# Layer 0 of a graph network: chunks turned so that one scan goes over five or ten features, and ScalarE turns the sums back

## The chip, the cores and the metric

The kernel runs on one core of a Trainium2 chip. The metric is the device time of one execution in microseconds (us); less is better. The core has five engines that run side by side, each with its own queue of instructions in a fixed order: TensorE (PE), VectorE (DVE), ScalarE (ACT), GpSimd (POOL) and SyncE (SP). Transfers between the device memory (DRAM) and the on-chip memory (SBUF) are issued from the queues of SP, ACT and POOL. PSUM is the small memory that PE writes and that DVE and ACT can also read and write.

## The reference

Four graph layers follow each other on 12500 nodes with 64 features and 200000 edges, sorted by destination. Layer 0, the one that is changed, computes per edge a message and per node a mean:

```python
h = jnp.maximum(_layernorm(x), 0.0)
msg = node_feats[src] + edge_feats                      # node_feats = h, edge_feats [200000, 64]
agg_sum = jax.ops.segment_sum(msg, dst, num_segments=N)
agg_mean = agg_sum / jnp.maximum(deg, 1.0)[:, None]
h = (1.0 + eps[0]) * node_feats + agg_mean
h = jax.nn.relu(_batchnorm(h @ W1 + b1, gamma1, beta1))
h = jax.nn.relu(_batchnorm(h @ W2 + b2, gamma2, beta2))
```

The other layers also gather rows by `src` and sum them by `dst`; they are not changed.

## The kernel before

**Sums by scan.** The edges are sorted by destination, so all edges of a node form a run. A range of edges is laid out as 128 partitions with TS slots each. For one feature, a scan along the slots of a partition adds up a run: `state = on * state + m`, where `on` (`goes_on`) is 1 where the edge has the same destination as the one before it, else 0. The last slot of a run then holds the node's sum. The scanned values go to a table `run_sums_0` in DRAM, and later the row of each node's last edge is gathered from it. `carry_on` adds what goes over from one partition to the next, by a scatter on POOL (L307).

**Two passes in layer 0.** `Runs` objects hold the slots. `cold` has 1001 slots per partition in 21 chunks of 48: POOL gathers the `h` row of each edge's source (L299, one indirect transfer per slot, 128 rows of 64 values, tile `m_src`, `rows_ahead = 3` buffers), SP loads the edge features (`m_edge`, pieces of 16 slots), ACT copies eight slots of them to PSUM (`ps_e`, L1519, one buffer), DVE adds them (L1520), and scans the chunk (L792). `hot` has the first 578 slots per partition in 19 chunks of 32: SP loads only edge features (`m_hot`), and DVE scans them; what the source rows contribute there is computed with matrix products of 0/1 blocks (below). A chunk lies in SBUF as slots by features, so the 48 (or 32) values of one feature are 64 values apart, and there are 64 scans per chunk, one per feature:

```python
for d in range(D):
    nc.vector.tensor_tensor_scan(m[:, :nt, d], on, m[:, :nt, d],
        0.0 if before is None else before[:, d : d + 1], op0=ALU.mult, op1=ALU.add)
```

`before` (L834 for cold, L1585 for hot) is the chunk's last slot, which the next chunk starts from. The mask `on` is copied to PSUM by ACT (`ps_masks`, L785), 240 or 256 slots at a time. Then ACT's queue issues the chunk's store to `run_sums_0` (L837, L1586).

**Beside the cold chunks.** `edge_pass` loops over the cold chunks, and after each it lets four other works go on as far as they are due: the hot chunks (`hot_features`, due evenly over the first six cold chunks), `counts.work` (100 counts for degrees and run ends: ACT L930 and L946, DVE L931, PE L938), the zeroing of a table (`by_edge<-zeros`, 195 transfers on ACT's queue), and `build` of 13 blocks. `build` unpacks edges (L1212 to L1244, all between cold chunks 4 and 6), and then makes one-hot tiles on DVE (`part_is`, `place_is`, L1324 and L1332), multiplies them on PE (`ps_a`, L1368), and casts them on ACT into a block (L1382). `sums_of_block` then loads the split source rows in tiles of 14 (`split_rows`, L1302, `JA = 14`, seven per block, two buffers), multiplies them by the block on PE (`ps_h`, L1304), and DVE adds up three parts (`hot_rows`, L1313). Each unit of the next block takes along one tile of these sums.

**Order.** Within an engine the order of instructions is fixed when the kernel is built, and works are interleaved there: an instruction that waits holds all behind it on its engine. Tiles with one buffer (`bufs=1`) are written again only when all readers of their last contents are done.

**End of the stage.** After cold chunk 20, `carry_on` runs, POOL scatters its rows, and then gathers `sum` rows, with which the first matrix products of layer 0 begin.

Of the kernel before, what the change touches and what calls it, by code (L numbers as in the profile page):

```python
# [18 lines left out]
P = 128  # L19
D = 64  # L20
# [5 lines left out]
J = 98  # L26
# [28 lines left out]
JA = 14  # L55
# [105 lines left out]
def kernel(  # L161
# [30 lines left out]
    nc = tc.nc  # L192
# [527 lines left out]
    class Runs:  # L720
# [1 line left out]

        def __init__(self, keep, scratch, psum, edges, name, size, row0=0):
# [7 lines left out]
            self.src_i = edges.sources(keep, name)  # L733
            self.dst_i, dst_f, before_f = edges.destinations(scratch, name)
            self.dst_f = dst_f

            self.goes_on = keep.tile([P, self.TS], F32, name=f"{name}_goes_on")
# [10 lines left out]
        def first_runs(self, keep, pool, psum):  # L748
# [25 lines left out]
            nc.vector.memset(self.carry[:, 1, :1], 0.0)  # L774
            nc.vector.tensor_mul(self.carry[:, 1, 1:], one[:, : P - 1], self.carry[:, 0, 1:])

        def mask(self, psum, t0, nt):


            at = t0 % self.mask_width  # L780
            if at == 0:
                n = min(self.mask_width, self.TS - t0)
                if psum is not None:
                    self.on = psum.tile([P, 512], F32, name="ps_on")
                nc.scalar.copy(self.on[:, :n], self.goes_on[:, t0 : t0 + n])  # L785
            return self.on[:, at : at + nt]

        def scan(self, m, on, before, nt):


            for d in range(D):
                nc.vector.tensor_tensor_scan(  # L792
                    m[:, :nt, d],
                    on,
                    m[:, :nt, d],
                    0.0 if before is None else before[:, d : d + 1],
                    op0=ALU.mult,
                    op1=ALU.add,
                )

        def edge_pass(self, table, load, message, beside=(), masks=1, ends=1, late=False):
# [3 lines left out]
            with ExitStack() as stack:  # L805
                pool = stack.enter_context(tc.tile_pool(name="edges", bufs=2))
                psum = stack.enter_context(tc.tile_pool(name="ps_edge", bufs=1, space=PSUM))
                self.psum = psum
# [16 lines left out]
                for c, (t0, nt) in enumerate(self.chunks):  # L825
                    on, loaded = ahead
                    if c + 1 < len(self.chunks):
                        ahead = load_chunk(*self.chunks[c + 1])
                    m = message(pool, psum, loaded, on, t0, nt)
                    if not masks:  # L830
                        on = self.mask(None, t0, nt)
                    self.scan(m, on, before, nt)
# [154 lines left out]
    class Ordered(Edges):  # L987
# [56 lines left out]
        def prepare(self, keep, edge_keep):  # L1044

            pool = self.scratch_pool
            with self.scratch, tc.tile_pool(name="ps_prepare", bufs=1, space=PSUM) as psum:
                self.cold = Runs(edge_keep, pool, psum, cold_edges, "cold", self.SIZE_0, self.COLD)
                self.hot = Runs(edge_keep, pool, psum, hot_edges, "hot", self.HOT_SIZE_0)
# [247 lines left out]
        def sums_of_block(self, pool, psum, block, b):  # L1297

            p = psum.tile([P, 3, D], F32, name="ps_h")
            for j0 in range(0, J, JA):  # L1300
                a = pool.tile([P, JA, 3, D], BF16, name="split_rows")
                nc.sync.dma_start(a, self.split[:, j0 : j0 + JA])  # L1302
                for j in range(j0, j0 + JA):
                    nc.tensor.matmul(  # L1304
                        p.rearrange("p k d -> p (k d)"),
                        block[:, j, :],
                        a[:, j - j0].rearrange("p k d -> p (k d)"),
                        start=j == 0,
                        stop=j == J - 1,
                    )  # L1310
                yield
            r = pool.tile([P, D], F32, name="hot_rows")
            nc.vector.tensor_reduce(r, p.rearrange("p k d -> p d k"), AX.X, ALU.add)  # L1313
            nc.sync.dma_start(self.hot_sums_0[b * CB : (b + 1) * CB], r)
# [168 lines left out]


        SIZE_0 = 48
        HOT_SIZE_0 = 32

        def layer0(self, h0):
            PIECE = 16
# [22 lines left out]

            def message(pool, psum, s, on, t0, nt):
                e = cold.pop(t0)
                for b in range(0, nt, TE):
                    nb = min(TE, nt - b)
                    p = psum.tile([P, TE * D], F32, name="ps_e").rearrange("p (t d) -> p t d", d=D)
                    at = b % PIECE
                    self.copied = nc.scalar.copy(p[:, :nb, :], e[b // PIECE][:, at : at + nb, :])  # L1519
                    nc.vector.tensor_add(s[:, b : b + nb, :], s[:, b : b + nb, :], p[:, :nb, :])  # L1520
                t1 = t0 + nt
                if t1 < self.cold.TS:
                    cold[t1] = pieces(pool, t1, min(self.SIZE_0, self.cold.TS - t1))
                return s

            def built(c):

# [5 lines left out]
            with self.first_stack:  # L1533
                self.prepare(self.count_keep, self.edge_keep)
                with tc.tile_pool(name="ps_masks", bufs=1, space=PSUM) as psum:
                    on = psum.tile([P, 2, 256], F32, name="ps_masks")
                    for k, runs in enumerate((self.hot, self.cold)):
                        runs.on = on[:, k, :]
                        runs.mask_width = 256 // runs.size * runs.size
# [28 lines left out]
        def hot_features(self):  # L1568

            runs = self.hot  # L1570
            with tc.tile_pool(name="hot_features", bufs=2) as pool:
# [31 lines left out]
        def layer1(self, a_table, b_table):  # L1603
# [5 lines left out]
            def load(pool, on, t0, nt):  # L1609
# [16 lines left out]
                self.all.scan(d, on, prior[0], nt)  # L1626
# [353 lines left out]
```

## Time and profile before

| | us |
|---|---|
| median of 3 runs (6052.3 to 6059.85) | 6053.1 |
| the profiled execution | 6051.88 |
| its span, first to last instruction | 6050.0 |
| first gather of layer 0 starts | 74.2 |
| last gather of layer 0 starts | 1392.2 |
| scatter that ends the layer's edge pass starts | 1459.5 |

In the stretch from 60 to 1480 us the scans of cold chunks take 283 us of DVE (1216 of 128x48 at 291 ns, 64 at 231, 64 of 128x41 at 277), counted one by one, and the scans of hot chunks 211 us.

How to read the views: a group is a line of the kernel with an engine and an operation; after the count come its busy time in us, the mean ns of one, and the idle time of the engine just before it with what ended that idle time. The waits list who waited for whom, in us, times, and the longest. In the timeline each piece has its start and duration in us; the part in brackets is the idle time before it. In the slices, each digit is the busy share in tenths in one of 40 equal parts of the span (151 us each). `PEld` is PE's weight load. Instructions on DVE overlap by some tens of ns, so that scans in a row take less than the sum of their durations.

### The profile page before, as it was taken

What the parts mean: (1) busy time and instruction counts of PE and PEld (TensorE: products, weight loads), DVE (VectorE), ACT (ScalarE), POOL (GpSimd) and SP (SyncE); (2) the same over time, 40 slices, a digit from 0 to 9 for tenths busy, and PEclk for the clock granted to TensorE, in tenths of its full rate; (3) what the DMA queues carried; (4) which work ended last, traced back from release to release, by engine and by line L of the source; (5) the groups of instructions that cost most, each with busy time, mean ns of one, the idle gap of its engine ahead of it and who ended that gap; (6) DMA issues with size and microseconds to landing.
All of it is one profiled execution on the core that took longest, in us unless ns stands there. A gap on an engine that the chain in (4) does not pass through costs nothing. (4 is left out here: it accounts for less than half of the span.)

```text
span 6050.0 us, 59020 instructions
## 1 busy us (share of the span) xinstructions
PE 3615.4 (60%) x16229; PEld 1736.4 (29%) x16229; DVE 3500.5 (58%) x12505; ACT 1680.2 (28%) x3570; POOL 4155.7 (69%) x4378
## 2 busy tenths in 40 slices
PE   3412665664646145455555556559995899659995
PEld 2101443442232011111111111134444444344444
DVE  6799988775525278677877777642333223352333
ACT  2421465554327032233444434320001000020001
POOL 5777677774436767777777777567776677647775
PEclk9999887776655577666666666559996899769995
DMA  6573477785113244344444444439995899659993
GB/s 207 203 268 99 158 262 257 256 282 174 38 65 105 77 153 141 119 140 159 147 147 149 164 145 137 146 97 385 386 386 184 328 385 386 245 192 386 386 381 125
DMA packets 452864, 1277.60 MB, mean 211 GB/s; under 512 B 136677, under 2 KB 146855, under 8 KB 427434
## 3 DMA queue, kind: packets, MB, share of 16 engines
q1 hardware_dynamic: 247274, 925.85, 41.6%
q0 software_dynamic: 139872, 143.10, 9.8%
q10 hardware_dynamic: 65376, 204.79, 8.8%
q8 instruction: 130, 2.13, 0.1%
q14 instruction: 212, 1.74, 0.1%
HBM read 859.98 MB, written 418.12 MB: 211 GB/s over the span
## 5 line engine op out<-in xcount | busy, mean ns | idle before, releaser
L299 POOL DMA_INDIRECT m_src<-ordered_a_table,all_src_i x1563 | 1475.6, 944 | 502.3 <-issue 458.9
L792 DVE TENSOR_TENSOR_SCAN m_src<-ps_on,before,m_src 128x32 f32<-128x32 f32 (+3 forms) x4032 | 805.2, 281 | 1041.5 <-DMA m_src<-ordered_h,later_src_i 346.1
L299 POOL DMA_INDIRECT m_src<-ordered_h,cold_src_i x1001 | 963.8, 963 | 318.8 <-issue 297.1
L1382 ACT CAST block<-ps_a 128x294 bf16<-128x294 f32 (+3 forms) x1801 | 859.7, 535 | 773.3 <-PE ps_a L1368 707.3
L1368 PE MATMUL ps_a<-place_is,part_is 128*128 128x98 bf16 (+4 forms) x2671 | 736.5, 375 | 472.1 <-DVE place_is L1332 204.1
L1703 PE MATMUL ps_upper<-blocks,upper 128*128 128x512 bf16 x3822 | 873.5, 380 | 154.5 <-DMA blocks<-blocks 133.2
L703 PE MATMUL ps_e<-w1e,et 64*128 64x512 f32 x392 | 284.3, 813 | 513.0 <-DVE m_src L714 512.9
L1703 PEld LDWEIGHTS <-upper 128*128 128x128 bf16 x3822 | 377.1, 99 | 619.2 <-issue 231.9
L1324 DVE TENSOR_TENSOR part_is<-ps_iota,part 128x512 bf16<-128x512 f16 (+2 forms) x665 | 424.4, 638 | 212.7 <-PE ps_a L1368 192.3
L1368 PEld LDWEIGHTS <-part_is 128*128 128x128 bf16 x2671 | 286.4, 121 | 902.6 <-issue 334.0
L299 POOL DMA_INDIRECT m_src<-ordered_scaled,later_src_i x430 | 405.7, 944 | 187.0 <-issue 129.5
L299 POOL DMA_INDIRECT m_src<-ordered_h,later_src_i x430 | 405.8, 944 | 158.7 <-issue 129.8
L938 PE MATMUL ps_row<-digits,on 128*128 128x391 bf16 x1016 | 299.8, 434 | 352.2 <-DVE on L931 135.8
L299 POOL DMA_INDIRECT m_src<-ordered_v,later_src_i x430 | 405.8, 944 | 146.1 <-issue 129.5
L1712 PE MATMUL ps_lower<-blocks,lower 128*64 128x512 bf16 x3822 | 464.5, 382 | 0.0
L1332 DVE TENSOR_SCALAR place_is<-ps_iota,place 128x294 bf16<-128x294 f16 (+3 forms) x1199 | 446.7, 428 | 0.0
L792 DVE TENSOR_TENSOR_SCAN m_dst<-ps_on,last_dst,m_dst 128x64 f32<-128x64 f32 (+1 forms) x1536 | 372.5, 323 | 0.0
L714 DVE TENSOR_TENSOR m_src<-m_src,ps_e 128x512 f32<-128x512 f32 x196 | 133.7, 682 | 390.1 <-DMA m_src<-ordered_a_table,all_src_i 207.1
L711 PE MATMUL ps_e<-m_dst,ident 128*128 128x512 f32 x392 | 281.2, 807 | 122.0 <-DVE m_dst L792 122.0
L1726 ACT COPY sum<-ps_upper 128x512 f32<-128x512 f32 x39 | 22.8, 585 | 1009.9 <-PE ps_upper L1703 878.3
L792 DVE TENSOR_TENSOR_SCAN m_src<-ps_masks,before,m_src 128x48 f32<-128x48 f32 (+1 forms) x1280 | 273.0, 290 | 0.2
L1712 PEld LDWEIGHTS <-lower 128*64 128x64 bf16 x3822 | 193.2, 109 | 255.6 <-issue 115.7
(364 smaller groups left out, 4413.2 us busy)
## 6 DMA issues: line engine op xcount, KB each, us to landing
blocks<-blocks SPq DMA_DIRECT2D x273, 1792.0 KB
blocks<-block SPq DMA_DIRECT2D x52, 3136.0 KB
split_rows<-split SPq DMA_DIRECT2D x91, 672.0 KB
by_edge<-zeros ACTq DMA_DIRECT2D x195, 256.0 KB
m_dst<-by_edge SPq DMA_DIRECT2D x24, 2048.0 KB
run_sums<-m_src ACTq DMA_DIRECT2D x24, 2048.0 KB
run_sums<-m_src ACTq DMA_DIRECT2D x39, 1024.0 KB
run_sums<-m_src ACTq DMA_DIRECT2D x20, 1536.0 KB
```

What stands on the lines that cost most here:

```text
L299: nc.gpsimd.indirect_dma_start(out=t, out_offset=None, in_=table, in_offset=bass.IndirectOffsetOnAxis(ap=idx, axis=0),)
L703: nc.tensor.matmul(p[:, :nb, :], et[: nb * EF], w1e[: nb * EF, : nb * D], start=True, stop=more is None,)
L711: nc.tensor.matmul(p[:, :nb, :], ident, more[:, b : b + nb, :], start=False, stop=True)
L714: nc.vector.tensor_add(m[:, b : b + nb, :], m[:, b : b + nb, :], p[:, :nb, :])
L792: nc.vector.tensor_tensor_scan(m[:, :nt, d], on, m[:, :nt, d], 0.0 if before is None else before[:, d : d + 1], op0=ALU.mult, op1=ALU.add,)
L938: nc.tensor.matmul(p[:, b, :W], on[:, 0, :], self.digits[:, i, v : v + W], start=i == 0, stop=i == 1,)
L1324: nc.vector.tensor_tensor(to[:, :n, :], iota[:, None, :m].to_broadcast([P, n, m]), of[:, t : t + n][:, :, None].to_broadcast([P, n, m]), o ...
L1332: nc.vector.tensor_scalar(place[:, k, :], iota[:, : J * w], self.place[:, t + k : t + k + 1], None, op0=ALU.is_equal,)
L1368: nc.tensor.matmul(out[:, :, (k - first) * w : (k - first + 1) * w], part[:, k, :], place[:, k, a * w : z * w], start=begin, stop=left == 0,)
L1382: nc.scalar.copy(block[:, a:z, c : c + wide], out)
L1703: nc.tensor.matmul(upper, self.upper[:, j].rearrange("p a d -> p (a d)"), a[:, :, j - j0, :], start=j == 0, stop=j == J - 1,)
L1712: nc.tensor.matmul(lower[k * D : (k + 1) * D], self.lower[:, j, :], a[:, :, j - j0, :], start=j < 2, stop=j >= J - 2,)
```

## The change

- `cold` and `hot` of layer 0 call `several_features`. Their chunks are scanned in a tile `turned` (64 x 48 values, one buffer, shared by hot and cold), in which a feature's slots lie side by side.
- Cold: DVE's adds write into `turned` in place of `m_src`, with slots 4 bytes and features 192 bytes apart. Hot: ACT copies the loaded chunk into `turned` first.
- One scan then goes over 5 features of 48 slots (cold, 13 scans per chunk, twelve of 240 values and one of 192) or 10 features of 24 slots (hot, 7 scans). The mask holds the chunk's `goes_on` once per feature, with 0 at each first slot; what the chunk before carries over is added into the first slot by one DVE operation (`before` times `goes_in`).
- ACT writes this mask for every chunk, and copies the scanned `turned` back into the chunk's own tile, from which it is stored.
- Hot chunks have 24 slots in place of 32: 25 chunks in place of 19.
- `split_rows` tiles have 7 rows in place of 14, so there are 14 transfers per block in place of 7, and each unit takes half as many products along.
- The sources of the hot edges, which nothing reads, are not loaded.

```diff
+        def several_features(self, keep, on):
+            self.features = on.shape[1] // self.size
+            self.on = on
+            self.goes_in = keep.tile([P, len(self.chunks)], F32, name=f"{self.name}_goes_in")
+            nc.vector.tensor_copy(self.goes_in, self.goes_on[:, :: self.size])
+            nc.vector.memset(self.goes_on[:, :: self.size], 0.0)
+
+        def by_feature(self, pool, nt):
+            m = pool.tile([P, D * Ordered.SIZE_0], F32, name="turned", bufs=1)
+            return m[:, : D * nt].rearrange("p (d t) -> p t d", t=nt)
...
         def mask(self, psum, t0, nt):
+            if self.features > 1:
+                on = self.on[:, : self.features * nt]
+                nc.scalar.copy(
+                    on.rearrange("p (d t) -> p d t", t=nt),
+                    self.goes_on[:, None, t0 : t0 + nt].to_broadcast([P, self.features, nt]),
+                )
+                return on
...
-        def scan(self, m, on, before, nt):
+        def scan(self, m, on, before, t0, nt):
...
+            if before is not None:
+                k = t0 // self.size
+                nc.vector.scalar_tensor_tensor(
+                    m[:, 0, :], before, self.goes_in[:, k : k + 1], m[:, 0, :],
+                    op0=ALU.mult, op1=ALU.add,
+                )
+            flat = m.rearrange("p t d -> p d t").rearrange("p d t -> p (d t)")
+            for d in range(0, D, self.features):
+                s = slice(d * nt, min(d + self.features, D) * nt)
                 nc.vector.tensor_tensor_scan(
-                    m[:, :nt, d], on, m[:, :nt, d],
-                    0.0 if before is None else before[:, d : d + 1],
+                    flat[:, s], on[:, : s.stop - s.start], flat[:, s], 0.0,
...
-                    self.scanned = nc.vector.tensor_copy(before, m[:, nt - 1, :])
+                    self.scanned = nc.vector.tensor_copy(before, turned[:, nt - 1, :])
+                    if self.features > 1:
+                        nc.scalar.copy(m[:, :nt, :], turned)
...
-            for j0 in range(0, J, JA):
-                a = pool.tile([P, JA, 3, D], BF16, name="split_rows")
+            n = JA // 2
+            for j0 in range(0, J, n):
+                a = pool.tile([P, n, 3, D], BF16, name="split_rows")
...
-        HOT_SIZE_0 = 32
+        HOT_SIZE_0 = 24
...
             def message(pool, psum, s, on, t0, nt):
                 e = cold.pop(t0)
+                turned = self.cold.by_feature(pool, nt)
...
-                    nc.vector.tensor_add(s[:, b : b + nb, :], s[:, b : b + nb, :], p[:, :nb, :])
+                    nc.vector.tensor_add(turned[:, b : b + nb, :], s[:, b : b + nb, :], p[:, :nb, :])
...
-                    runs.scan(m, runs.mask(None, t0, nt), before, nt)
+                    turned = runs.by_feature(self.cold.pool, nt)
+                    nc.scalar.copy(turned, m[:, :nt, :])
+                    runs.scan(turned, runs.mask(None, t0, nt), before, t0, nt)
                     before = pool.tile([P, D], F32, name="before")
-                    nc.vector.tensor_copy(before, m[:, nt - 1, :])
+                    nc.vector.tensor_copy(before, turned[:, nt - 1, :])
+                    nc.scalar.copy(m[:, :nt, :], turned)
```

More of the change, by code (lines that the diff above doesn't have):

```diff
@@ L720, with __init__ @@
     class Runs:
-        def __init__(self, keep, scratch, psum, edges, name, size, row0=0):
+        def __init__(self, keep, scratch, psum, edges, name, size, row0=0, sources=True):
             self.edges = edges
@@ L732, in __init__ @@
             self.chunks = [(t, min(size, self.TS - t)) for t in range(0, self.TS, size)]
-            self.src_i = edges.sources(keep, name)
+            if sources:
+                self.src_i = edges.sources(keep, name)
             self.dst_i, dst_f, before_f = edges.destinations(scratch, name)
             self.dst_f = dst_f
+            self.features = 1
             self.goes_on = keep.tile([P, self.TS], F32, name=f"{name}_goes_on")
@@ L786, in mask @@
             return self.on[:, at : at + nt]
-        def scan(self, m, on, before, nt):
-            for d in range(D):
+        def scan(self, m, on, before, t0, nt):
+            if self.features == 1:
+                for d in range(D):
+                    nc.vector.tensor_tensor_scan(
+                        m[:, :nt, d],
+                        on,
+                        m[:, :nt, d],
+                        0.0 if before is None else before[:, d : d + 1],
+                        op0=ALU.mult,
+                        op1=ALU.add,
+                    )
+                return
+            if before is not None:
+                k = t0 // self.size
+                nc.vector.scalar_tensor_tensor(
+                    m[:, 0, :],
+                    before,
+                    self.goes_in[:, k : k + 1],
+                    m[:, 0, :],
+                    op0=ALU.mult,
+                    op1=ALU.add,
+                )
+            flat = m.rearrange("p t d -> p d t").rearrange("p d t -> p (d t)")
+            for d in range(0, D, self.features):
+                s = slice(d * nt, min(d + self.features, D) * nt)
                 nc.vector.tensor_tensor_scan(
-                    m[:, :nt, d],
-                    on,
-                    m[:, :nt, d],
-                    0.0 if before is None else before[:, d : d + 1],
+                    flat[:, s],
+                    on[:, : s.stop - s.start],
+                    flat[:, s],
+                    0.0,
                     op0=ALU.mult,
@@ L807, in edge_pass @@
                 psum = stack.enter_context(tc.tile_pool(name="ps_edge", bufs=1, space=PSUM))
-                self.psum = psum
+                self.pool, self.psum = pool, psum
                 if masks:
@@ L831, in edge_pass @@
                         on = self.mask(None, t0, nt)
-                    self.scan(m, on, before, nt)
+                    turned = m
+                    if self.features > 1:
+                        m, turned = m
+                    self.scan(turned, on, before, t0, nt)
                     before = pool.tile([P, D], F32, name="before")
-                    self.scanned = nc.vector.tensor_copy(before, m[:, nt - 1, :])
+                    self.scanned = nc.vector.tensor_copy(before, turned[:, nt - 1, :])
+                    if self.features > 1:
+                        nc.scalar.copy(m[:, :nt, :], turned)
                     stores.append((self.slots(table, t0, nt), m[:, :nt, :]))
@@ L1048, in prepare @@
                 self.cold = Runs(edge_keep, pool, psum, cold_edges, "cold", self.SIZE_0, self.COLD)
-                self.hot = Runs(edge_keep, pool, psum, hot_edges, "hot", self.HOT_SIZE_0)
+                self.hot = Runs(edge_keep, pool, psum, hot_edges, "hot", self.HOT_SIZE_0, sources=False)
                 src_i = all_edges.sources(pool, "all")
@@ L1299, in sums_of_block @@
             p = psum.tile([P, 3, D], F32, name="ps_h")
-            for j0 in range(0, J, JA):
-                a = pool.tile([P, JA, 3, D], BF16, name="split_rows")
-                nc.sync.dma_start(a, self.split[:, j0 : j0 + JA])
-                for j in range(j0, j0 + JA):
+            n = JA // 2
+            for j0 in range(0, J, n):
+                a = pool.tile([P, n, 3, D], BF16, name="split_rows")
+                nc.sync.dma_start(a, self.split[:, j0 : j0 + n])
+                for j in range(j0, j0 + n):
                     nc.tensor.matmul(
@@ L1523, in message @@
                     cold[t1] = pieces(pool, t1, min(self.SIZE_0, self.cold.TS - t1))
-                return s
+                return s, turned
             def built(c):
@@ L1537, in layer0 @@
                     for k, runs in enumerate((self.hot, self.cold)):
-                        runs.on = on[:, k, :]
-                        runs.mask_width = 256 // runs.size * runs.size
+                        runs.several_features(self.edge_keep, on[:, k, :])
                     self.cold.edge_pass(
@@ L1625, in load @@
                     nc.scalar.copy(d[:, 0, :], first)
-                self.all.scan(d, on, prior[0], nt)
+                self.all.scan(d, on, prior[0], t0, nt)
                 prior[0] = pool.tile([P, D], F32, name="last_dst")
```

## The prediction

> **What bounds the kernel now.** I read the page's busy shares and slices first, to find what is full in the stage that the change touches (about 74 to 1460 us, slices 1 to 10 of 40):
>
> ```profile
> PE 3615.4 (60%) x16229; PEld 1736.4 (29%) x16229; DVE 3500.5 (58%) x12505; ACT 1680.2 (28%) x3570; POOL 4155.7 (69%) x4378
> ...
> DVE  6799988775525278677877777642333223352333
> ACT  2421465554327032233444434320001000020001
> POOL 5777677774436767777777777567776677647775
> ```
>
> DVE reads 9 in slices 3 to 5, but POOL reads 7 throughout. So I asked for POOL's waits and its timeline in this stage:
>
> ```profile
> POOL m_src L299 <- issue: 297.1, 975, 0.3
> POOL m_src L299 <- DVE place_is L1324: 15.0, 8, 9.0
> ```
>
> ```profile
> 678.42 0.98 POOL L299 DMA_INDIRECT m_src<-ordered_h,cold_src_i  x1 [8.97 <-DVE place_is L1324]
> ...
> 742.38 0.94 POOL L299 DMA_INDIRECT m_src<-ordered_h,cold_src_i  x1 [4.17 <-DVE place_is L1324]
> ...
> 1392.22 0.94 POOL L299 DMA_INDIRECT m_src<-ordered_h,cold_src_i  x1 [0.30 <-issue]
> 1459.52 1.62 POOL L307 DMA_INDIRECT run_sums<-rest,cold_first_end  x1 [66.35 <-DVE inv_deg L496]
> ```
>
> The reader is to see that POOL issues one gather each 1.25 us (0.94 busy and 0.30 of issue), 1001 for `m_src` and 27 for `keys`, from 74.2 to 1393.2 us: 1028 x 1.249 = 1284 of 1319 us. The scans can give back only what POOL waits for: 9.0 + 4.2 = 13 us for a free buffer (a gather of chunk c+3 needs chunk c stored), and 66.4 us between the last gather and the scatter that ends the stage. Everything else that DVE saves is hidden behind POOL.
>
> How far DVE is behind follows from the timeline: from a cold chunk's last gather to its `before` copy (L834) it takes 36 us at chunk 3, 84 at 5, 127 at 6, 129 at 7 (here POOL waits), then 30 at 13, 44 at 15, 60 at 17, 65 at 18, 89 at 19, 63 at 20. So there are two stretches that count: the early one, with the hot chunks between the cold ones, which ends in POOL's waits, and the late one from chunk 13, which builds up the tail.
>
> **Prices.** These groups (busy sum, then mean ns of one) and pieces of the timeline carry them:
>
> ```profile
> L792 DVE TENSOR_TENSOR_SCAN m_src<-ps_on,before,m_src 128x32 f32<-128x32 f32 x2304 | 407.8, 257 | 1019.8 <-DMA m_src<-ordered_v,later_src_i 340.3 <-DMA m_src<-ordered_h,later_src_i 340.0 <-DMA m_src<-ordered_scaled,later_src_i 339.5
> L792 DVE TENSOR_TENSOR_SCAN m_src<-ps_on,before,m_src 128x64 f32<-128x64 f32 x1472 | 358.9, 326 | 3.5 <-ACT m_src L1634 3.5
> L1313 DVE TENSOR_REDUCE hot_rows<-ps_h 128x64 f32<-128x192 f32 x13 | 4.6, 356 | 33.8 <-PE ps_h L1304 33.7
> L1378 DVE TENSOR_REDUCE most<-ps_a 128x1 f32<-128x392 f32 x7 | 3.9, 560 | 0.9 <-PE ps_a L1368 0.9
> L1634 ACT ACTIVATE m_src<-m_src 128x4096 f32<-128x4096 f32 x24 | 87.0, 3626 | 63.4 <-DMA m_src<-ordered_a_table,all_src_i 42.6 <-DVE m_src L714 20.7 <-issue 0.2
> ```
>
> ```profile
> 91.15 7.79 DVE L792 TENSOR_TENSOR_SCAN m_hot<-ps_masks,m_hot 128x32 f32<-128x32 f32 x64 [9.41 <-DMA m_hot<-in_edge_attr_dram]
> ...
> 305.76 11.32 DVE L792 TENSOR_TENSOR_SCAN m_hot<-ps_masks,before,m_hot 128x32 f32<-128x32 f32 x64
> ...
> 1133.08 12.60 DVE L792 TENSOR_TENSOR_SCAN m_src<-ps_masks,before,m_src 128x48 f32<-128x48 f32 x60
> ...
> 1441.63 12.51 DVE L792 TENSOR_TENSOR_SCAN m_src<-ps_masks,before,m_src 128x41 f32<-128x41 f32 x64
> ```
>
> *Scans.* One element costs (326 - 257) / 32 = 2.16 ns. In a row, 64 scans of 32 with 0.0 as the start take 7.79 us, 122 ns each, 53 of them fixed; with a start from memory 11.32 us, 177 each. A scan of 240 is then 53 + 240 x 2.16 = 571 ns. A cold chunk goes from 64 x 0.210 = 13.5 us (60 in 12.60) to 12 x 0.571 + 0.468 = 7.3, saving 6.2; the last (41 slots) from 12.5 to 6.4. A hot chunk of 24 goes to 6 x 0.571 + 0.260 = 3.7; before it was 11.3 for 32 slots, 8.5 for 24. In all DVE loses about 125 us (cold) and 120 (hot), and gets 44 small operations that add `before` into the first slot (about 0.15 each in a row, 7 us).
>
> *ScalarE.* A copy costs (3626 - 1044) / 3072 = 0.84 ns per element (1044 is the mean of the 128x1024 casts): 2.76 us to turn a cold chunk back, 1.47 for 1536 elements of a hot one, there and back. 21 x 2.76 + 25 x 2 x 1.47 and some 40 more masks at 0.37 make about 144 us more on ACT, which has 43 us busy of 60 in its fullest late stretch (1282 to 1342).
>
> *Strided access.* No row has ACT or DVE touching SBUF at full rate one 4-byte element at a time, 96 or 192 bytes apart, as the turned tile asks (the adds write so, the copies write or read so). The scans of before step 256 bytes, but at two cycles per element, which could hide a second one. The nearest row is L1313, which reads PSUM 256 bytes apart: 192 elements in 356 ns against 392 side by side in 560 (L1378) is 1.02 ns per element, no surcharge. I take none (below nothing is excluded, an element per cycle is the best seen), and doubling the per-element part is the other end: adds 0.68 to 1.2 us, copies 2.76 to 5.3 and 1.47 to 2.75.
>
> The Trainium skill, SBUF — State Buffer, section "Door 1: The DMA port swizzle", speaks against the change: SBUF has lines of 16 bytes, and an access that goes to a new line each time pays a penalty, free strides ending at 4 fp32 values. It gives no price; taken as a doubling it would make the whole sum +57 us, against -35 with no surcharge as in L1313, which is PSUM; no row here shows SBUF.
>
> *One turned tile for hot and cold.* It adds a wait at each step: DVE's scans wait for ACT's copy in, ACT's copy out for the scans, and the next chunk, hot or cold, for that copy. Behind the waiting DVE stand the `on` differences, one-hots and adds; behind ACT the counts, `ps_e` copies and block casts. For a hot chunk the round is 1.47 + 0.15 + 3.7 + 0.2 + 1.47, with mask 0.37 and store issue 0.33: 7.7 us, against 8.5. So the early stretch gains far less than DVE's busy time says: 25 x 0.8 = 20 us of hot, and 6 x (6.2 - 2.8) = 20 of cold, up to 40 before chunk 6, if nothing stands in between. ACT's counts stand in between (3 us each by their rows), so I take back only half of POOL's 13: 6 us.
>
> *Late stretch.* From chunk 14 to 19 DVE's scans stand in one chain with PE and ACT (while chunk 18 is scanned ACT waits 12.99 us for `ps_row`). Each chunk saves 6.2, and pays for the copy nothing to all of 2.8: 3.4 to 6.2, taken 4.8, x 6 = 29 us. The last chunk saves 6.1 of scans, 2.05 of waiting for `hot_rows` (in the order of the changed kernel the last of these comes behind `before` and the carry), and pays 2.4 for the copy before its store: 5.7. The tail can't shrink below some 17 us (one landing, an add, 6.4 scans, 2.4 copy, 5.4 from the scan's end to the scatter), so 35 of 66 is within its limit.
>
> *Halved `split_rows`.* 182 transfers of 336 KB in place of 91 of 672, on SP's queue ahead of `m_edge` loads; PE waited 94 us for them in the stage (53 between 1040 and 1430). If only bytes count it costs nothing, if each transfer takes as long as before the last block's sums take 23 us more, which the order puts beside the first gathers of `sum`. Taken: 6 us. Hot chunks of 24 move the same bytes, at no cost. Three fewer `hot_src_i` loads stand ahead of the first gather, worth 0 to 2 us (1.5 us of SP's issue): taken nothing.
>
> Sum: -6 - 29 - 5.7 + 6 = -35. The profiled execution took 6051.9 us (span 6050.0 and 1.9 around it), 1.2 below the median of 6053.1: 6053.1 - 35 = 6018.
>
> **The rivals.**
> *Slower: turning costs double* (strided SBUF). A hot round is 10.3 us against 8.5, x 25 = 45 us; a cold chunk early pays 3.2 for adds and 5.3 for the copy against 6.2 saved, 2.3 x 6 = 14. Chunk 6, for which POOL waits already, ends 59 us later, and so do all gathers after it. Late, a chunk nearly breaks even and the tail gains 8. With 6 for `split_rows`: +57, 6110. In terms of the surcharge y (1 is double) the early stretch changes by -40 + 99y and the late one by -35 + 27y; with the early gain worth only 6, it turns slower from y of about 0.55. For it: DVE is full in the early slices and 25 rounds pass through two queues that must take their turn. Against: L1313.
>
> *No change: the saving becomes waiting.* ACT's extra 3.1 us per chunk lands in the late chain in full, its copy stands behind block casts, and the handoff gives DVE idle time for busy time. Then a chunk saves 2, the tail 12 + 5.7, `split_rows` takes 6 or more, POOL's waits stay: -10, 6043, and to 6060 if the halved tiles cost more. For it: PE's in-order waits (94 us for `split_rows`) don't depend on scans at all.
>
> That a long scan costs more per element than the short ones show is a small rival within these: at 2.6 ns a cold chunk gets 3072 x 0.44 = 1.4 us less than its 6.2.
>
> **How the numbers follow.** A difference under 0.2%, 12 us, can't be told from none. My forecast, 5990 to 6041: 0.52; about no change, 6041 to 6065: 0.16; slower, 6065 to 6125: 0.32. The range 5988 to 6110 leaves out the last part of the slower case and what lies below the bound of the tail. Faster by over 12 us is all of the forecast and a little of the second case, 0.54; within, 0.13; slower, the third and a little of the second, 0.33.
>
> **What would show it.** Right: gathers still every 1.25 us; scans of 240 near 0.6 us; the idle time of POOL before the last scatter near 30 us; copies of 3072 near 2.8. Wrong: adds into the turned tile near 1.2 us or copies near 5; POOL waiting much more than 13 us between 450 and 750; the lag at chunk 19 still near 89 with cheap copies, which would put the late stretch on PE and ACT alone.

## The result and the profile after

The changed kernel takes 6220.8 us (median of 4 runs, 6217.1 to 6223.7) beside 6052.7 of the kernel before in the same comparison: a ratio of 1.0275, 95% interval 1.0257 to 1.0292, or 168 us slower. The profiled execution has a span of 6220.6 us. (Eight of the experiments' runs belong to two series in which the kernel before itself took 9523 and 9529 us, for a reason that stays open; seven of them were repeated elsewhere, and of these series only the rows of single instructions are used.)

The same lines of the page as before, POOL's waits from 60 to 1700 us (in us, times, longest), and its timeline around the end of the stage:

```profile
PE 3686.5 (59%) x16229; PEld 1752.6 (28%) x16229; DVE 3306.2 (53%) x10447; ACT 1996.6 (32%) x3679; POOL 4153.7 (67%) x4378
...
DVE  6348865665451557877777767743223222352223
ACT  3776365566241613223344444421000100020001
POOL 5777577763423767777777777756776677647775
```

```profile
POOL run_sums L307 <- DMA split_rows<-split: 134.7, 1, 134.7
POOL m_src L299 <- DMA run_sums<-m_src: 91.6, 5, 44.4
...
POOL sum L299 <- DMA all_before<-in_dst_dram: 12.8, 1, 12.8
```

```profile
1612.50 1.61 POOL L307 DMA_INDIRECT run_sums<-rest,cold_first_end  x1 [134.74 <-DMA split_rows<-split]
...
1631.71 0.98 POOL L299 DMA_INDIRECT sum<-run_sums,last_row  x1 [12.75 <-DMA all_before<-in_dst_dram]
```

In the kernel before, the first `sum` gather came here:

```profile
1463.98 0.97 POOL L299 DMA_INDIRECT sum<-run_sums,last_row  x1 [2.84 <-DVE r L1402]
```

DVE did lose its work: its digits in slices 2 to 5 fell from 7 9 9 9 to 3 4 8 8, 194 us less in all. POOL's digits hardly show the loss (6 3 4 2 for 7 4 4 3 in slices 9 to 12); its waits and its timeline do. Three things moved the end of the stage. POOL waited 101 us for buffers (91.6 for the store of a chunk, 9.4 for ACT) where it had waited 13, and the last gather ends at 1477.8 in place of 1393.2. From there to the scatter it waited 134.7 in place of 66.4. And from the scatter to the first `sum` gather it now takes 19 us where it took 4.5. That first gather comes at 1631.7 in place of 1464.0: the whole 168 us are lost by then (85, 68 and 15).

The prices that the prediction worked out, by group (busy sum, mean ns of one, then idle time before):

```profile
L838 DVE TENSOR_TENSOR_SCAN turned<-ps_masks,turned 128x240 f32<-128x240 f32 x384 | 215.8, 631 | 6.5 <-ACT turned L1636 3.8 <-ACT ps_masks L798 1.9
L1573 DVE TENSOR_TENSOR turned<-m_src,ps_e 128x512 f32<-128x512 f32 x125 | 127.4, 1019 | 57.5 <-ACT ps_e L1572 20.9 <-ACT m_hot L1640 19.6 <-DMA m_src<-ordered_h,cold_src_i 9.2
L885 ACT COPY m_src<-turned 128x3072 f32<-128x3072 f32 x20 | 108.0, 5398 | 86.0 <-DVE turned L838 41.1 <-DMA by_edge<-zeros 28.2 <-DMA m_src<-ordered_h,cold_src_i 16.7
L1636 ACT COPY turned<-m_hot 128x1536 f32<-128x1536 f32 x24 | 96.3, 4014 | 2.7 <-ACT ps_masks L798 1.4 <-DVE cold L1277 0.2
L827 DVE SCALAR_TENSOR_TENSOR turned<-before,hot_goes_in,turned 128x64 f32<-128x64 f32 x24 | 9.0, 375 | 125.3 <-ACT turned L1636 125.3
```

The scans are at their price: one lasts 631 ns, but in a row each overlaps the next, and the thirteen of a cold chunk take 7.13 us (7.3 worked out). The copies are not: 5.40 us against 2.76, and 4.01 against 1.47. DVE stands idle 125 us in front of the hot chunks' first operation, until ScalarE has turned the chunk in.

How far DVE is behind (the lag), from a cold chunk's last gather to its `before` copy, in us by chunk:

| kernel | 3 | 5 | 6 | 7 | 10 | 13 | 16 | 19 | 20 |
|---|---|---|---|---|---|---|---|---|---|
| before | 36 | 84 | 127 | 129 | 59 | 30 | 58 | 90 | 63 |
| after | 98 | 148 | 189 | 178 | 82 | 86 | 130 | 158 | 123 |

So there are two losses: an early one, up to chunk 7, and a late one. The kernel before caught up from 129 to 30 between chunks 7 and 13; the changed kernel stops at 82 and falls behind again.

### The profile page after: what moved, and what is told of

It reads as the page before. It is cut to its first block, busy times and chain, and to the rows that moved or that the text cites. A ratio compares the mean times of both kernels' runs of the same rounds, so it can differ in the third digit from the quotient of the medians.

```text
span 6220.6 us, 57262 instructions
## 1 busy us (share of the span) xinstructions
PE 3686.5 (59%) x16229; PEld 1752.6 (28%) x16229; DVE 3306.2 (53%) x10447; ACT 1996.6 (32%) x3679; POOL 4153.7 (67%) x4378
## 5 line engine op out<-in xcount | busy, mean ns | idle before, releaser
L1420 PE MATMUL ps_a<-place_is,part_is 128*128 128x98 bf16 (+4 forms) x2671 | 757.7, 386 | 492.9 <-DVE place_is L1384 206.9
L989 PE MATMUL ps_row<-digits,on 128*128 128x391 bf16 x1016 | 332.3, 468 | 464.7 <-ACT whole L1000 233.3
L989 PEld LDWEIGHTS <-on 128*128 128x128 bf16 x1016 | 127.7, 128 | 623.3 <-issue 568.2
L1356 PE MATMUL ps_h<-split_rows,block 128*128 128x192 bf16 x1274 | 202.2, 321 | 152.3 <-DMA split_rows<-split 145.9
```

Of the source, the lines that this page charges most:

```text
L989: nc.tensor.matmul(p[:, b, :W], on[:, 0, :], self.digits[:, i, v : v + W], start=i == 0, stop=i == 1,)
L1356: nc.tensor.matmul(p.rearrange("p k d -> p (k d)"), block[:, j, :], a[:, j - j0].rearrange("p k d -> p (k d)"), start=j == 0, stop=j == J - 1,
L1420: nc.tensor.matmul(out[:, :, (k - first) * w : (k - first + 1) * w], part[:, k, :], place[:, k, a * w : z * w], start=begin, stop=left == 0,)
```

## Experiments

Each time is the median of a kernel's runs, the ratio is to the kernel before in the same comparison.

### What a step in SBUF costs

A kernel that only copies and adds, three times each form, one after the other on one engine. The two kinds of line:

```diff
+    for _ in range(3): nc.scalar.copy(near[:, :1536], far[:, : 6144 : 4])
+    for _ in range(3): nc.scalar.copy(near[:, : 1536].rearrange("p (t d) -> p t d", d=64),
+        far[:, : 1536].rearrange("p (d t) -> p t d", t=24)[:, :24, :])
```

> A kernel of its own that leaves out the whole network: it runs only ScalarE and VectorE copies of 128x1536 fp32 from SBUF to SBUF, and VectorE adds of 128x512 with one operand in PSUM, each three times in a row, with the one side contiguous and the other at a step of 1 to 65 elements. Theory (a step in SBUF has a price that was taken as nothing): ScalarE 1.47 us contiguous, some 2.6 at a step of 48 elements (192 bytes; from 5.40 us for 3072) and 4.0 at 24 (96 bytes), alone as in the kernel; VectorE's add 0.68 contiguous and 1.02 at 48. If a new 16-byte line is what costs, all steps from 4 elements on cost the same. Rival (the copies are slowed by what else runs on SBUF at that time: scans, transfers): alone they take near 1.5 us at any step, the adds near 0.68.

Its groups: L208 to L211 are steps of 1, 2, 3 and 4 elements, L219, L220 and L224 of 24, 25 and 48, L231 writes at 24; L286, L288 and L290 are adds that write at 1, 24 and 48:

```profile
L208 ACT COPY near<-far 128x1536 f32<-128x1536 f32 x3 | 4.4, 1471 | 19.2 <-DVE near L206 19.2
L209 ACT COPY near<-far 128x1536 f32<-128x1536 f32 x3 | 4.7, 1567 | 0.1
L210 ACT COPY near<-far 128x1536 f32<-128x1536 f32 x3 | 6.7, 2236 | 0.1
L211 ACT COPY near<-far 128x1536 f32<-128x1536 f32 x3 | 8.7, 2889 | 0.1
L219 ACT COPY near<-far 128x1536 f32<-128x1536 f32 x3 | 12.1, 4017 | 0.1
L220 ACT COPY near<-far 128x1536 f32<-128x1536 f32 x3 | 8.7, 2902 | 0.1
L224 ACT COPY near<-far 128x1536 f32<-128x1536 f32 x3 | 8.3, 2772 | 0.1
L231 ACT COPY far<-near 128x1536 f32<-128x1536 f32 x3 | 12.1, 4017 | 0.1
L286 DVE TENSOR_TENSOR far<-near,edge 128x512 f32<-128x512 f32 x3 | 2.1, 686 | 0.1
L288 DVE TENSOR_TENSOR far<-near,edge 128x512 f32<-128x512 f32 x3 | 4.3, 1433 | 0.1
L290 DVE TENSOR_TENSOR far<-near,edge 128x512 f32<-128x512 f32 x3 | 3.0, 1014 | 0.1
```

The copy at a step of 24 takes 4017 ns alone and 4014 in the changed kernel, so nothing else that runs on SBUF slows it: the rival falls. A step of 8 bytes is nearly free, one of 12 bytes costs half as much again, and from 16 bytes on a copy takes about double or more, reading or writing. The Trainium skill, SBUF — State Buffer, section "Door 1: The DMA port swizzle", has lines of 16 bytes, a penalty for each new one, and strides that are free up to 4 fp32 values. The runs agree on the penalty and give its price, but not on the last: 4 values apart takes 2889 ns against 1471, and 3 apart 2236. A new line each time is not all that costs, either: a step of 24 elements (96 bytes) takes 2.73 times as long as none, while 25 takes 1.97.

### The changed kernel without steps: flat2

Against the changed kernel; the turned tile keeps the chunk's layout, so the scans run over values of other features, and layer 0's sums are not the reference's. Instructions, sizes and waits stay.

```diff
-            return m[:, : D * nt].rearrange("p (d t) -> p t d", t=nt)
+            return m[:, : D * nt].rearrange("p (t d) -> p t d", d=D)
...
-            flat = m.rearrange("p t d -> p d t").rearrange("p d t -> p (d t)")
+            flat = m.rearrange("p t d -> p (t d)")
```

> The changed kernel with the same instructions, sizes, order and waits, but the turned tile laid out slot by slot like the chunk, so that no copy and no add has a step; the scans then run over other data, and the sums of layer 0 are not those of the reference. Theory 1 (the price of steps is the cause): hot copies 1.5 us, cold copies 2.8, POOL's waits for buffers near 13 us, the tail before the scatter under 70: 6010 to 6060. Theory 2 (one turned tile, whose steps go through two queues, is the cause): POOL still waits 60 us or more, 6130 or more. Theory 3 (the halved split_rows hold the tail): waits for buffers gone, but the tail stays 110 to 135: 6090 to 6130.

9404.4 us, 0.9875 of the 9523 that the kernel before took there; the copies took 1.42 and 2.73 us on average, and nothing else can be read from it. Run again elsewhere:

> The kernel of run flat once more, since there the kernel before itself took 9523 us, with long waits for no engine of the trace. The price of a step is settled by the sweep (16 bytes or more double a copy, 96 bytes make it 2.7 times as long); what it did to the end is not. Theory 1 (the price of steps is the whole cause): copies of 1.4 and 2.7 us, POOL's waits for buffers near 13 us, the tail before the scatter under 70: 6010 to 6060. Theory 2 (one turned tile whose steps go through two queues): POOL still waits 60 us or more: 6130 or more. Theory 3 (halved split_rows hold the tail): waits gone but the tail stays 110 to 135: 6090 to 6130.

6171.4 us, 1.0198 (1.0181 to 1.0215), with copies of 2.76 and 1.47 us as predicted. The steps are worth 53 us (168 to 115), so theory 1 is a part, and 115 remain. By its numbers theory 2 came true (POOL waits 63 us for buffers, and 6171 is over 6130), but flat64 below has the same single tile and 7 us of such waits. The wait before the scatter is 103.7 us, near theory 3's 110. The lag is 16 at chunk 3 and 32 at chunk 5, so the early loss is gone. But ACT's timeline and POOL's then show this:

```profile
610.93 2.75 ACT L885 COPY m_src<-turned 128x3072 f32<-128x3072 f32 x1
613.59 0.91 ACT L997 ACTIVATE up_to<-ps_row,node 128x782 bf16<-128x782 f32 x1
...
659.71 0.33 ACTq L888 DMA_DIRECT2D run_sums<-m_src  x1
660.08 0.16 ACT L1000 COPY whole<-ps_row 128x1 f32<-128x1 f32 x1 [45.49 <-issue]
```

```profile
655.07 0.94 POOL L299 DMA_INDIRECT m_src<-ordered_h,cold_src_i  x1 [0.30 <-issue]
656.32 1.65 POOL L307 DMA_INDIRECT run_sums<-rest,hot_first_end  x1 [0.30 <-issue]
```

Chunk 6 was copied back at 613.7, but its store (L888) issues at 659.7, and ACT stands still for 45.5 us. The store goes to the table to which POOL's hot scatter adds (L307), and the scatter stands behind 426 gathers in POOL's fixed order; its input `rest` was ready at 543.1. The trace shows that ACT's queue waits before this store for the semaphore of the scatter's transfer: the last update comes at 659.64, and the wait ends at 659.67. In the kernel before, chunk 6 was scanned only at 672.6, after the scatter (667.8), so nothing showed it. An early gain thus ends at a gate that gathers of 1.25 us set. What moving the scatter would bring was not tried.

Behind the gate flat2 has lags of 116, 105, 103, 142 and 117 us at chunks 7, 10, 13, 16 and 19: the late loss is there without any step.

### The halved split_rows alone: before_halved2 and halved4b

```diff
-            for j0 in range(0, J, JA):
-                a = pool.tile([P, JA, 3, D], BF16, name="split_rows")
+            for j0 in range(0, J, JA // 2):
+                a = pool.tile([P, JA // 2, 3, D], BF16, name="split_rows")        # halved4: bufs=4
...
```

> The kernel before with split_rows tiles of 7 in place of 14, nothing else. Theory 1: 6 us, at most 23 more: 6053 to 6076, the wait before the scatter 66 to 85 us. Theory 3 (each transfer has a fixed time, and 14 of them in a row per block stand before the last adds and in the tail): the wait before the scatter grows to 110 or more, 6100 to 6120.

1.0067 of the 9523 us there. Run again elsewhere:

> The kernel before with split_rows tiles of 7 in place of 14 once more, on a chip where the kernel before takes 6053. Theory 1: +0 to 23 us, 6053 to 6076, the wait before the scatter 66 to 85. Theory 3 (the halved transfers hold PE before the last chunk and in the tail): the wait before the scatter 110 or more, 6100 to 6120. In the slow runs it was 1.0067 of before; the same ratio here would be 6093.

6121.3 us, 1.0110 (1.0092 to 1.0128): 64 us more: a little over theory 3's 6120, and far from theory 1. The early lags are as before; from chunk 8 on they grow beyond it (95 against 60 at chunk 17), and the wait before the scatter is 104.8 us (110 or more expected). The expectation had the last block's sums in mind; the trace shows the loss in all blocks, and behind the scatter too, where the first `sum` gather comes 32 us later in place of 4.5.

> before_halved2 with four split_rows tiles of 7 in place of two, the same bytes as two tiles of 14. If the halving costs 64 us because each transfer has a fixed time and PE, in order, waits for them two at a time (PE waited 161 us for split_rows between 760 and 1560 us, against 94 with tiles of 14): PE's wait falls to 90 or less and the time to 6040 to 6065. If it is the order of PE's work with twice as many pieces: 6100 to 6125 as with two tiles.

0.9998 of the 9529 us there, where before_halved had 1.0067. Run again elsewhere:

> halved4 once more, on a chip where the kernel before takes 6053. Two transfers in flight as the cause: PE's wait for split_rows between 760 and 1560 us at 90 or less (161 with two tiles of 7), 6040 to 6065. Order and number of pieces as the cause: 6100 to 6125.

6048.7 us, 0.9999 (0.9989 to 1.0008): with four tiles of 7 the halving costs nothing. PE's wait between 760 and 1560 us, first with two tiles of 7, then with four:

```profile
PE ps_h L1304 <- DMA split_rows<-split: 161.4, 92, 12.2
```

```profile
PE ps_h L1304 <- DMA split_rows<-split: 92.9, 51, 12.4
```

With two tiles of 14 it was 93.9. So what counted was not bytes nor the number of transfers, but how many bytes are on their way ahead of PE: two small tiles are used up before the next lands, and everything behind PE's waiting product waits along.

### Only hot, only cold: hot_only2 and cold_only

hot_only2 leaves `message` and the cold scan as before and has tiles of 14; cold_only leaves the hot chunks unturned:

```diff
-                        runs.several_features(self.edge_keep, on[:, k, :])
+                        if k:      # cold (hot_only2) - in cold_only the two branches change places
+                            runs.on = on[:, k, :]
+                            runs.mask_width = 256 // runs.size * runs.size
+                        else:
+                            runs.several_features(self.edge_keep, on[:, k, :])
...
```

> The changed kernel with only the hot chunks turned (24 slots, one turned tile of 24 slots); cold chunks are added and scanned as before, split_rows tiles are 14 again. Theory 1: each hot chunk takes 4.0 + 0.4 + 3.7 + 0.2 + 4.0 = 12.3 us and more in its round against 8.5 before, x 25 = 95 us; POOL's waits rise from 13 to 80 or more, the tail stays near 66: 6110 to 6150. Theory 3: without the halving most of the loss is gone, 6060 to 6090.

0.9868 of the 9523 us there. Run again elsewhere:

> Only the hot chunks turned, split_rows 14, once more, on a chip where the kernel before takes 6053. The hot round is 12.3 us and more against 8.5, x 25: some 95 us later at the end of the hot chunks; 27 us of it is covered, since ScalarE waited so long there for the hot scatter, which stands behind 432 gathers on POOL's queue. The built order of counts and blocks is as before (153 changes). Theory 1: POOL's waits 60 to 90, the tail near 66: 6090 to 6135. If the stretch behind the scatter catches up (the lag fell from 129 to 30 there in the kernel before), only POOL's waits count and the tail stays; if it gains nothing of it, 6053 to 6070.

6063.5 us, 1.0022 (1.0013 to 1.0031), below the expected 6090 and in its last range. The lag at chunk 6 is 154 against 127, POOL waits 33 us for buffers in place of 13, and then the stretch catches up as in the kernel before (27 at chunk 13) and the tail is 62.3: the loss is POOL's extra wait. So hot copies of 4 us cost 15 us here, where the late stretch can catch up. (The 27 us of the expectation are no wait for the hot scatter: in the kernel before they end at 584.8 with DVE's `rest`, L867, and the scatter comes at 667.8.)

Theory O in the next expectation, O for order, is that of the next section: with other scans on DVE, the built order of the other engines changes.

> The changed kernel with the hot chunks scanned as before (24 slots, 64 scans, no copies); cold chunks turned, split_rows 7. 25 hot chunks of 64 scans take some 256 us of DVE against 215 before. Built order as in the changed kernel (91 changes). Theory O with the halving: +64 for the halved tiles and the late stretch as slow as in flat2 or slower (strided copy 5.4): the lag at chunks 10 to 14 over 80, 6150 to 6200. Theory 1 (only the price of the hot copies): 6060 to 6100.

6192.3 us, 1.0237 (1.0221 to 1.0252): as theory O expected. With only the cold chunks turned, and the halved tiles, 144 of the 168 us are there. The lag is 89 at chunk 10 and 94 at 13.

### What holds the late stretch: the order (flat64, after64b)

What PE does from 880 to 1060 us, one line per 60 us, worked out from its timeline (c a group of `ps_row` products of the counts, a of `ps_a` of the blocks, h of `ps_h`):

```
before  cacacacacacacacaaaaccacccaacacacachchahchacacac
        aaaahachcachchcchcacacacacacacacacacaaaachcahch
        chahhcahcahchahcacacacacacacaaaaaaahah
flat2   ahaacccchchahhhchhchchchhchchcacacacaaaaaa
        aaaaaaaccccaccaccccccacacaahahahaaaaaaaaaha
        hcchchcachchchachcahhchhccccccacacaaaaaaaaaaaa
```

Before, a count and a block take turns; in flat2 they come in rows of their own. A count is a round of PE and ACT, 2.6 us for each half (1.47 of products, 1.10 of ACT), in which each waits for the other; a block is a round of DVE, PE and ACT. In rows, the one no longer fills the waits of the other. flat2's timeline shows DVE in such a row of counts:

```profile
971.33 0.22 DVE L982 TENSOR_TENSOR on<-on 128x128 bf16<-128x128 bf16 x1 [5.00 <-ACT on L981]
...
976.62 0.22 DVE L982 TENSOR_TENSOR on<-on 128x128 bf16<-128x128 bf16 x1 [5.06 <-ACT on L981]
```

The orders are fixed when a kernel is built, and there they can be counted: from the end of the hot chunks on, leaving out the sums h, PE's products change to a count 152 times in the kernel before, 148 in before_halved2, 153 in hot_only2, but 88 in flat2, 91 in cold_only and 84 in the changed kernel. What these three share, and the others do not have, is 13 scans per cold chunk in place of 64. So the cold chunk was scanned feature by feature again, in the turned tile:

```diff
-            for d in range(0, D, self.features):
-                s = slice(d * nt, min(d + self.features, D) * nt)
+            step = self.features if self is edges_hot[0] else 1      # edges_hot: the hot Runs
+            for d in range(0, D, step):
+                s = slice(d * nt, min(d + step, D) * nt)
...
```

> flat2 (turned tile without steps, so other sums) with the cold chunk scanned by 64 scans of 48 in place of 13 of 240; hot chunks keep 7 scans of 240. DVE gets some 2 to 3 us more per cold chunk, 21 chunks. In the built order PE's counts (ps_row) and blocks (ps_a) alternate again as in the kernel before (140 changes to a count between chunks 6 and 20, against 88 in flat2 and 148 in before_halved). Theory O (the long scans change the order that the builder gives PE, DVE and ACT, so that counts and blocks stand in blocks one behind the other and no longer beside each other): faster than flat2 by 25 us or more in spite of the longer scans, the lag at chunks 12 to 14 back near 50 in place of 100: 6100 to 6145. Theory W (the single turned tile and its waits hold the late stretch): DVE's extra makes it slower: 6171 to 6220.

6102.0 us, 1.0082 (1.0067 to 1.0098): 61 us less than flat2's 115, with more work on DVE. The lag is 51 at chunks 12 and 13. DVE's wait for ACT's `on` between 760 and 1300 us, in flat2 and in flat64:

```profile
DVE on L982 <- ACT on L981: 113.1, 20, 14.5
```

```profile
DVE on L985 <- ACT on L984: 18.2, 14, 5.8
```

(In the kernel before it is 1.3.) So it went as theory O expected. The single turned tile with its waits and cheap copies, the halved tiles and the gate (ACT stands still for 48.6 us here, too) are in both kernels, and are not what sets them 61 us apart.

One rival stands beside the order: the TensorE clock that the profile shows as granted, as a share of full speed. Between 760 and 1400 us it was 0.76 in the kernel before, 0.74 in before_halved2, 0.73 in flat64, 0.68 in flat2 and 0.68 in the changed kernel, and the same products of counts, blocks and sums kept PE busy for 738 us in flat64 and 778 in flat2. If all of this stood in the chain, 40 of the 61 us would be longer products (an estimate from these two sums). Whether the rows of counts bring the lower clock with them is not shown: no run changes the order and leaves the scans as they are.

> The changed kernel as it is (strided copies, right sums), with the cold chunks scanned by 64 scans of 48 in the turned tile. In flat that took 69 us away (6171 to 6102), where the built order went from 88 to 140 changes to a count; here it goes from 84 to 115 only, with 44 of 180 counts in rows of four or more (96 of 186 before). Theory O: 30 to 60 us below the changed kernel's 6221, 6160 to 6190. If the copies alone hold the late stretch: 6215 to 6250, since DVE has 2 to 3 us more per cold chunk.

0.9956 of the 9529 us there. Run again elsewhere:

> after64 once more, on a chip where the kernel before takes 6053. Theory O (order): 30 to 60 us below the changed kernel's 6221, 6160 to 6190. Copies alone: 6215 to 6250.

6188.8 us, 1.0224 (1.0207 to 1.0242), at the edge of what theory O expected: 26 us better (168 to 142 over the kernel before), where the order was restored in part (115 changes; DVE waits 58 us for `on`, in the changed kernel 96).

### The 96-byte step alone: after_pad2

```diff
-        HOT_SIZE_0 = 24
+        HOT_SIZE_0 = 25
```

> The changed kernel with hot chunks of 25 in place of 24 slots, so that the features of a hot chunk lie 100 bytes apart in place of 96 (scans of 250, 24 chunks). By the sweep a copy of 1536 at a step of 25 elements takes 2.90 us in place of 4.02: 1600 at 3.0 us, two per chunk, 24 x 2 x 1.0 = some 50 us of ScalarE's path in the early stretch, the lag at chunk 6 down from 189 to about 150 and POOL's early waits from 70 to 30. The order is as clumped as before (87 changes): the late stretch and the tail stay. 6175 to 6205; no change (6215 or more) if the gate at the hot scatter takes it all.

0.9907 of the 9529 us there. Run again elsewhere:

> after_pad once more, on a chip where the kernel before takes 6053: hot copies 3.0 us in place of 4.0, the lag at chunk 6 down from 189 to about 150, POOL's early waits from 70 to 30; the late stretch and the tail stay as clumped: 6175 to 6205, or 6215 and more if the gate at the hot scatter takes it all.

6173.5 us, 1.0198 (1.0183 to 1.0214). Hot copies take 2.97 us on average (1600 elements, the last one shorter) in place of 4.01 for 1536, the lag at chunk 6 is 123 (below the 150 expected), POOL waits 35 us for stores in place of 92. One slot more per chunk (and with it 24 chunks in place of 25) saves 54 us, as much as flat2 did by having no steps at all, although the cold copies still take 5.4 us.

### A version that beats both: start0

The prediction had noted that a scan that starts from memory takes 177 ns where one that starts from 0.0 takes 122. That needs no turning:

```diff
+            if t0 is not None and before is not None:      # layer 0 only
+                nc.vector.scalar_tensor_tensor(
+                    m[:, 0, :], before, self.goes_on[:, t0 : t0 + 1], m[:, 0, :],
+                    op0=ALU.mult, op1=ALU.add,
+                )
+                before = None
             for d in range(D):
...
```

> The kernel before, nothing turned: only the start of each scan in layer 0 is 0.0 in place of the value in before, which is added into the chunk's first slot by one operation (before times goes_on). In the trace of before 64 scans of 32 in a row took 7.79 us with 0.0 and 11.32 with a start from memory, 55 ns each: 3.5 us less per chunk and 0.35 for the add, 39 chunks, 120 us of DVE. POOL's 13 us of waits and part of the 66 us tail can come back: 6030 to 6053. If the built order or PE and ScalarE set the late stretch (143 changes to a count, against 152): 6050 to 6075.

6007.5 us, 0.9928 (0.9915 to 0.9942): 41 us faster than the kernel before, more than the 6030 to 6053 expected, and 213 faster than the changed one. In DVE's timeline 64 scans of a hot chunk take 7.81 us, and the wait at the end of the stage is 39 in place of 66:

```profile
290.13 7.81 DVE L798 TENSOR_TENSOR_SCAN m_hot<-ps_masks,m_hot 128x32 f32<-128x32 f32 x64
```

```profile
1417.40 1.61 POOL L307 DMA_INDIRECT run_sums<-rest,cold_first_end  x1 [39.40 <-DVE up_to_node L1458]
```

POOL's 13 us of waits for buffers are gone, which with 27 at the end of the stage is nearly all of the 41; the lag at chunk 13 is 18. Five `split_rows` tiles of 7 and no sources of the hot edges, on top of it:

> start0 (6007 us) with split_rows tiles of 7, five of them, and no load of the sources of the hot edges. If the halved tiles with more in flight let PE wait less than with two of 14: below start0, 5985 to 6005. If the number of transfers itself costs: 6010 to 6040.

0.9896 of the 9529 us there. Run again elsewhere:

> start0_h5 once more, on a chip where the kernel before takes 6053. halved4b took 6049 with four tiles of 7, no more than with two of 14, so the fifth tile and the smaller transfers are worth little: 5995 to 6010, start0 was 6007.

6010.6 us, 0.9925 (0.9911 to 0.9938): the same as start0.

## Why the prediction was wrong

The forecast was 6018, the range 5988 to 6110; the changed kernel took 6221. Against their own kernel before, the experiments stand in a row: halved tiles +64 (before_halved2), turning without steps and with nearly the old order +54 (flat64), the new order +115 (flat2), the steps +168 (the changed kernel). So the halving cost 64, the turning as it was meant gave back 11, the order (with the lower clock) cost 61 and the steps 53. The forecast had 6 for the halving, a gain of 41 from turning, and nothing for the other two, and the four differences, 58, 30, 61 and 53, are the 203 us between -35 and +168. The parts depend on each other (the order gave back only 26 in after64b, and hot copies of 4 us cost only 15 in hot_only2), so this is one way to divide the sum. The changed kernel with four `split_rows` tiles was not run.

- **Scans: right.** 7.1 us per cold chunk against 7.3 predicted.
- **"I take none" (strided access): the step that failed first.** The row it rested on, L1313, reads PSUM. In SBUF the copies cost 5.40 and 4.01 us (2.76 and 1.47 in the sum), the adds 1.02 (0.68). The sentence on the Trainium skill, SBUF — State Buffer, section "Door 1: The DMA port swizzle", had the right sign. Even the other end, a doubling, was too low for the hot copy: 2.75 against 4.01, since 96 bytes is a bad step.
- **"Halved `split_rows`: taken 6 us": mis-sized, 64.** It reckoned in bytes, and put a fixed time per transfer only on the last block. What was left out is that two tiles half as large also halve what is on its way; halved4b shows it.
- **"Each chunk saves 6.2 ... taken 4.8, x 6 = 29": not there.** From chunk 13 to 19 the lag grew by 60 us in the kernel before, by 75 with the halved tiles alone and by 72 in the changed kernel: 3 us came of the 29. The sum let the engines' order stand as it was and put shorter scans into it. Fewer DVE instructions gave counts and blocks another order, and between flat64 and flat2 that is worth 61 us, with the clock as an open part. The order was there to be seen in the built program.
- **Early stretch: right where copies are cheap.** 6 of POOL's 13 us were to come back; in flat64 7 us of such waits are left. The lag itself fell by more than the 40 us worked out (at chunk 6 to 68 in flat2 and 66 in flat64, from 127), and the gain ended at the gate of the hot scatter, which the prediction did not have. With copies of 4 us POOL waits 101 us.
- **The rivals.** "Turning costs double" named the mechanism of the early loss, but priced it with a late stretch that gains. "ACT's extra lands in the late chain" was not it with cheap copies: flat64 has them too, at 2.7 us, and is 61 us faster than flat2.

## What to carry to other kernels

Where a change alters how many instructions an engine has, look at the built order of all engines before adding up savings: work that took turns may come to stand in rows, here at up to 61 us. Price a strided access with a row from the same memory, and try the step one element longer: here that took a quarter off the copy. When a buffer is made smaller to make room, count the bytes that stay on their way, not the bytes that are moved.

## What the runs showed of the hardware

- ScalarE copies 1536 fp32 values per partition from SBUF to SBUF in 1.47 us; at a step of 8 bytes in 1.57, 12 bytes 2.24, 16 bytes 2.89, 192 bytes 2.77, 100 bytes 2.90 and 96 bytes 4.02, the same for reading and writing at 96 (sweep).
- VectorE's add of 512 values with one operand in PSUM takes 0.69 us, at an output step of 192 bytes 1.01 and at 96 bytes 1.43 (sweep).
- A VectorE scan that starts from a value in memory costs 55 ns more than one that starts from a constant: 64 of 32 elements took 11.32 us (the kernel before) and 7.81 (start0).
